# Moving part of the last layer's dense sums into the attention pass ahead of it

## The chip, the cores and the metric

One Trainium2 (trn2) chip, of which the kernel uses one core. Its engines are TensorE (PE; its weight loads are listed as PEld), VectorE (DVE), ScalarE (ACT), GpSimdE (POOL) and SyncE (SP), which issues the plain DMAs. The metric is the device time of one execution in microseconds; the median of the runs counts. Names such as L2227 are lines of the kernel before; in the changed kernel the lines behind the edit are up to 54 higher.

## The reference

Four layers of a graph network run over 6250 nodes of 256 features and 100000 random edges (`src`, `dst`, sorted by `dst`); after each layer the result is added to its input and normalised. Layers 0 and 1 are a mean aggregation and a dot-product attention. What bears on the change are the last two:

```python
# layer 2, twice: graph attention with 4 heads (edges and self-loops), exact GELU after each
h = (h_in @ W).reshape(n, Hh, Cc)
e = leaky_relu(alpha_s[src] + alpha_d[dst], 0.2)
alpha = softmax of e over the edges of each dst
out = segment_sum(h[src] * alpha[:, :, None], dst, n).reshape(n, Hh * Cc) + b
# layer 3, the last
msg_sum = segment_sum(x[src], dst, n)
cnt = segment_sum(ones, dst, n)
mean = msg_sum / maximum(cnt, 1.0)[:, None]
sage = mean @ W_l.T + b_l + x @ W_r.T
out = relu(relu(sage) @ W_ln.T + x)
# around each layer
x = _layernorm(x + layer(x))
```

## The kernel before

**Blocks.** The nodes form NB = 50 blocks of B = 125. The edges are laid out by target block, CM = 16 chunks of 128 edges each, with a few overflow chunks shared by 25 blocks (SH = 2). A *piece* is 4 chunks of one block in the attention passes (200 pieces a pass) and 6, 6 or 4 chunks in the last layer.

**The passes of layer 2.** `for layer in range(2)` runs two attention passes, the *first* and the *second pass* in the text. For each piece POOL gathers the rows of the source nodes from a table in DRAM (`gather`, L929, ten buffers `g`), DVE and ACT make the edge weights (L2152 to L2157) and scale the rows (L2160), DVE makes one-hot matrices of the targets (L938), and PE adds the rows into their targets (L2227). Once per block `keys2` makes one-hot columns `kb` on ACT (L947, L948) and spreads the targets' scores over the edges with 48 matmuls of 4 columns (L2185). `finish2` ends each pair of blocks. In the second pass it writes the new `x` times `W_l` as three bfloat16 parts to `x_table`, and, for the first ND = 24 blocks, `x` times `W_r` plus the bias, turned, to `xr_columns` (the *own-weight columns*).

**The last layer.** Its first 24 target blocks are summed densely: `a_table` holds, for each source node, a byte for each of 3000 targets, the count of edges between the two. `dense` walks over three groups of 8 target blocks (d = 0, 1, 2) and over the source blocks in pairs. For each pair it loads the rows of `x_table` (`xs`) and the counts of 1000 targets (`few`), ACT widens the counts to bfloat16 (`cnt`, L2343), and PE adds up: 3 parts x 2 halves of the features (DK = 2) x 2 *quarters* (q) of RW = 500 targets = 12 matmuls of 500 columns for each source block (L2393). At the end of a group `group3` multiplies by `rdeg_row` (one over the degree), adds the own-weight columns and hands over to `pair3`, which multiplies by `W_ln`. The other 26 target blocks (24 to 49) go by pieces with gathers from `x_table` (`piece3`, L929 and L963), among the dense steps.

**Where the counts come from.** `count_edges` makes `a_table` during the two passes of layer 2, with one-hot matrices on DVE (L1995) and matmuls of 500 columns (L2005); for each source block ACT evacuates two words of 1500 targets (L1981, L1982), both into one buffer `a_row`, which one store takes to DRAM.

**Order.** PE, DVE and ACT run in the order in which the program records them (`manual_schedule`); POOL and SP take theirs from the framework. The work of all pieces in flight is interleaved by *turns* (`Turns`): each piece, key block and finish is a generator that names the group in which it goes on. After turn t of a pass, `beside_2(t)` advances the counting:

```python
begin, until = (12 if layer == 0 else 0), len(made) - 12
share = COUNT_STEPS * (0.52 if layer == 0 else 0.5) / (until - begin)
```

In the last layer `beside_3` advances `dense` by RATE steps (yields of 12 matmuls) a turn, two for each pair of source blocks:

```python
RATE = 2 * len(order) / (0.9 * len(made))
```

with 75 pairs in `order` and 78 pieces in `made`. `LEAD` = 3 pairs are loaded ahead.

Of the kernel before, what the change touches and what calls it, by code (L numbers as in the profile page):

```python
# [17 lines left out]
P = 128  # L18
# [638 lines left out]
def gnn_stack_kernel(ctx: ExitStack, tc: tile.TileContext, ins, out):  # L657
# [33 lines left out]
    DK = D // P  # L691
# [21 lines left out]
    ND, RB, WORD = 24, 4, 3  # L713
    RW, NR = RB * B, ND // RB
# [10 lines left out]
    DC = max(c + n for _, c, n, _, _ in slots)  # L725
    COUNT_STEPS = NB * len(slots)
# [16 lines left out]
    with ExitStack() as fast:  # L743
# [47 lines left out]
        x_table = dram.tile([N, 3 * D], BF16, name="x_table_f")  # L791
# [837 lines left out]
        with tc.tile_pool(name="f0", bufs=1) as pool, tc.tile_pool(name="f0w", bufs=2) as work, tc.tile_pool(  # L1629
            name="f0v", bufs=1  # L1630
# [316 lines left out]
        def count_edges():  # L1947


            column = ap.tile([P, RW], F16, name="a_column", bufs=1)  # L1950
            nc.vector.scalar_tensor_tensor(
                column.rearrange("p (b n) -> p b n", n=B), iota[:, :RB, None].to_broadcast([P, RB, B]), float(B),
                iota_p[:, None, :B].to_broadcast([P, RB, B]), op0=ALU.mult, op1=ALU.add,
            )
            end, over = (
                ap.tile([P, 3, RW], BF16, name="a_hot", bufs=4).rearrange("p i j -> p (i j)").bitcast(F32)[:, : NB * DC]
                .rearrange("p (b c) -> p b c", c=DC) for _ in range(2)
            )
            nc.vector.tensor_copy(end, idx_s[:, :, :DC])
            unit = [ap.tile([P, NB, DC], F32, name=f"a_unit{w}", bufs=1) for w in range(NW)]  # L1960
            nc.vector.memset(unit[0], 1.0)
            for w in range(1, NW):
                nc.vector.memset(unit[w], 0.0)
            less = ap.tile([P, NB, DC], F32, name="a_less", bufs=1)
            nc.vector.tensor_copy(less, end)
            for r in range(1, NR + 1):
                nc.vector.tensor_single_scalar(over, end, float(r * RW), op=ALU.is_ge)
                nc.vector.scalar_tensor_tensor(less, over, -float(RW), less, op0=ALU.mult, op1=ALU.add)
                for w, by in ((r // WORD, 256.0 ** (r % WORD)), ((r - 1) // WORD, -(256.0 ** ((r - 1) % WORD)))):
                    if w < NW:  # L1970
# [3 lines left out]
            sts, rows, accs, hots, done = {}, {}, {}, {}, []  # L1974
            for k in range(len(steps) + 4):
                if done and done[0][2] <= k:
                    s, w, _ = done.pop(0)
                    if w == 0:
                        rows[s] = ap.tile([B, ND * B], U8, name="a_row", bufs=1)
                    word = ap.tile([B, RW], I32, name="a_word", bufs=1)  # L1980
                    nc.scalar.copy(word, accs.pop((s, w))[:B])  # L1981
                    nc.scalar.activation(  # L1982
                        rows[s][:, w * WORD * RW : (w + 1) * WORD * RW].rearrange("p (q j) -> p q j", q=WORD),
                        word.bitcast(U8).rearrange("p (j q) -> p q j", q=4)[:, :WORD, :], AF.Copy,
                        accum_out=counted[:B, s * NW + w : s * NW + w + 1],
                    )
# [12 lines left out]
                if 0 <= k - 1 < len(steps):  # L1999
                    s, w, c0, n, first, last = steps[k - 1]  # L2000
                    hot = hots.pop(k - 1)
                    if first:
                        accs[s, w] = apsum.tile([P, 512], F32, name="a_acc", bufs=2)[:, :RW]
                    for i in range(n):
                        nc.tensor.matmul(  # L2005
                            accs[s, w], sts[s][:, c0 + i, :], hot[:, i, :], start=(first and i == 0),
                            stop=(last and i == n - 1),
                        )
# [6 lines left out]
        counting = count_edges()  # L2015


        biases = [load_row(pool, ins[f"L2_gnn_b{i}"], f"bias{i}") for i in range(2)]
# [10 lines left out]
        for layer in range(2):  # L2029
# [7 lines left out]
            def finish2(b, layer):  # L2037
# [40 lines left out]
                else:  # L2078
# [164 lines left out]
            def beside_2(t):  # L2243
                if layer == 0 and t == 12:
                    next(counting)
                for _ in range(counts(t)):
                    next(counting, None)

            with tc.manual_schedule(engines={ENG.PE, ENG.DVE, ENG.Activation}):
                run_pass(turns, [(lambda a=a: piece2(*a)) for a in made], beside_2, keys2)  # L2250
                if layer:
                    for _ in counting:
                        pass


# [4 lines left out]
        with tc.tile_pool(name="f3g", bufs=5) as gp, tc.tile_pool(name="f3w", bufs=2) as work, tc.tile_pool(  # L2260
# [68 lines left out]
            order = [(d, s) for d in range(ND // (2 * RB)) for s in range(0, NB, 2)]  # L2329
            LEAD = 3  # L2330

            def load(k):
                d, s = order[k]
                xs = work.tile([B, 2, 3 * D], BF16, name="xs", bufs=LEAD + 1)
                move(nc.sync, xs, block_rows(x_table, s, 2))
                few = work.tile([B, 2, GW], U8, name="few", bufs=LEAD + 1)
                rows = a_table[s * B : (s + 2) * B, d * GW : (d + 1) * GW]
                move(nc.sync, few, rows.rearrange("(n p) d -> p n d", p=B))
                return xs, few

            def wide_counts(few):
                cnt = work.tile([B, 2, GW], BF16, name="cnt", bufs=3)
                nc.scalar.copy(cnt, few)  # L2343
                return cnt

            def pair3(b, sT, at):
# [26 lines left out]
            def dense():  # L2373
                loads = {k: load(k) for k in range(LEAD)}
                nexts = [wide_counts(loads[0][1])]
                for k, (d, s) in enumerate(order):
# [12 lines left out]
                    for i in range(2):  # L2389
                        for j in (2, 1, 0):  # L2390
                            for h in range(DK):
                                for q in range(2):
                                    nc.tensor.matmul(  # L2393
                                        accs[h][q], xs[:, i, j * D + h * P : j * D + (h + 1) * P],
                                        cnt[:, i, q * RW : (q + 1) * RW], start=(s + i == 0 and j == 2),
                                        stop=(s + i == NB - 1 and j == 0),
                                    )
# [85 lines left out]
```

## Time and profile before

| what | value |
|---|---|
| runs | 5936.43 us median of 3 (5924.23 to 5954.35) |
| profiled execution | 5892.39 us, span 5890.5 us |
| mean granted TensorE clock | 0.836 |
| PE, DVE, ACT, POOL busy | 4107.0, 3632.0, 2948.2, 3595.0 us |
| gathers (L929) of one attention pass | 800 |
| dense matmuls of the last layer (L2393) | 1800, 403.7 us busy |
| first, second attention pass, last layer | from about 2770, 3960, 5170 us |

The profile is of one execution. A group of instructions is read as: line, engine, operation, output <- inputs, shapes, count | busy us, mean ns of one | idle time of the engine just before them and what ended it. "issue" is time in which the engine waited for nothing that the profile shows. A line of a stretch gives busy us and the number of instructions of PE, PEld, DVE, ACT and POOL, then granted clock, DMA share and GB/s. Matmuls are pipelined: their mean duration overlaps, so that busy time by count gives the cost of one in a row.

### The profile page before, as it was taken

What the parts mean: (1) busy time and instruction counts of PE and PEld (TensorE: products, weight loads), DVE (VectorE), ACT (ScalarE), POOL (GpSimd) and SP (SyncE); (2) the same over time, 40 slices, a digit from 0 to 9 for tenths busy, and PEclk for the clock granted to TensorE, in tenths of its full rate; (3) what the DMA queues carried; (4) which work ended last, traced back from release to release, by engine and by line L of the source; (5) the groups of instructions that cost most, each with busy time, mean ns of one, the idle gap of its engine ahead of it and who ended that gap; (6) DMA issues with size and microseconds to landing.
All of it is one profiled execution on the core that took longest, in us unless ns stands there. A gap on an engine that the chain in (4) does not pass through costs nothing. (4 is left out here: it accounts for less than half of the span.)

```text
span 5890.5 us, 79635 instructions
## 1 busy us (share of the span) xinstructions
PE 4107.0 (70%) x25027; PEld 3010.6 (51%) x25027; DVE 3632.0 (62%) x9526; ACT 2948.2 (50%) x7453; POOL 3595.0 (61%) x3710
## 2 busy tenths in 40 slices
PE   0567788875777777773666766656776677769996
PEld 0355666663555566552554554544555555535554
DVE  7786666653767777773656656645766667613454
ACT  4015676882666676662454445533555555422331
POOL 5776666654666666653666666646666666556663
PEclk9788899997888888886777788777878878889998
DMA  6555565554666777763444444434545455477883
GB/s 157 141 165 159 157 158 155 153 149 143 204 204 206 208 211 210 207 189 86 132 135 134 135 137 136 133 101 123 146 139 140 138 147 140 118 197 221 235 238 102
DMA packets 409642, 940.75 MB, mean 160 GB/s; under 512 B 96973, under 2 KB 214331, under 8 KB 409211
## 3 DMA queue, kind: packets, MB, share of 16 engines
q0 software_dynamic: 221184, 670.83, 41.3%
q1 hardware_dynamic: 188026, 264.74, 15.3%
q8 instruction: 201, 3.29, 0.2%
q14 instruction: 231, 1.88, 0.1%
HBM read 848.02 MB, written 87.21 MB: 159 GB/s over the span
## 5 line engine op out<-in xcount | busy, mean ns | idle before, releaser
L929 POOL DMA_INDIRECT g<-hs_table_f,idx_d x1600 | 1527.6, 955 | 920.5 <-issue 453.1
L929 POOL DMA_INDIRECT g<-h_table_f,idx_d x800 | 802.0, 1002 | 435.2 <-issue 212.3
L2227 PE MATMUL ps<-g,st 128*125 128x260 f32 x3200 | 955.0, 445 | 116.6 <-issue 108.9
L929 POOL DMA_INDIRECT g<-kv_table_f,idx_s x784 | 744.8, 950 | 448.8 <-issue 289.4
L2160 DVE TENSOR_TENSOR g<-g,iota_p 128x1024 f32<-128x1024 f32 x400 | 488.4, 1221 | 654.6 <-ACT iota_p L2156 312.4
L2227 PEld LDWEIGHTS ps<-g,st 128*125 128x125 f32 x3200 | 712.7, 224 | 320.9 <-issue 151.0
L2185 PE MATMUL pe<-ad_parts,kb 125*128 125x4 bf16 x4800 | 220.1, 165 | 631.7 <-issue 543.1
L963 PE MATMUL ps<-g,st 128*128 128x256 bf16 (+1 forms) x3648 | 525.2, 300 | 136.3 <-issue 61.3
L929 POOL DMA_INDIRECT g<-x_table_f,idx_d x416 | 397.8, 956 | 289.3 <-issue 158.8
L963 PEld LDWEIGHTS <-st 128*128 128x128 bf16 x4104 | 427.8, 106 | 283.1 <-issue 130.3
L2185 PEld LDWEIGHTS <-kb 125*128 125x128 bf16 x4800 | 185.0, 99 | 721.8 <-issue 603.4
L1920 PE MATMUL ps<-g,st 128*125 128x264 f32 x1600 | 470.2, 442 | 28.1 <-issue 20.2
L947 ACT ACTIVATE kb<-kb,minus 125x512 bf16<-125x512 bf16 x600 | 426.2, 711 | 58.3 <-DMA g<-kv_table_f,idx 20.4
L948 ACT ACTIVATE kb<-kb,ones 125x512 bf16<-125x512 bf16 x600 | 432.6, 721 | 20.6 <-ACT kb L947 1.5
L2393 PE MATMUL d<-cnt,xs 125*128 125x500 bf16 x1800 | 403.7, 378 | 36.5 <-issue 20.4
L938 DVE TENSOR_TENSOR st<-iota_p,key_d 128x500 f32<-128x500 f32 (+1 forms) x550 | 410.6, 747 | 0.0
L1920 PEld LDWEIGHTS ps<-g,st 128*125 128x125 f32 x1600 | 344.9, 220 | 112.3 <-issue 28.9
L1903 DVE TENSOR_TENSOR prod<-g,qe 128x1024 f32<-128x1024 f32 x200 | 243.2, 1216 | 246.5 <-PE ps L1920 96.7
L2156 ACT ACTIVATE iota_p<-r 128x16 f32<-128x16 f32 (+2 forms) x504 | 90.9, 180 | 591.0 <-DVE e L2152 217.6
L1889 PE MATMUL qe<-q,kb 125*128 125x256 bf16 x2400 | 324.0, 288 | 65.6 <-issue 32.5
L1515 ACT ACTIVATE ob<-t_f,s_f 125x128 bf16<-125x128 f16 x800 | 310.3, 388 | 96.1 <-remote 65.1
L1889 PEld LDWEIGHTS <-kb 125*128 125x128 bf16 x2400 | 247.8, 103 | 141.6 <-issue 77.6
(458 smaller groups left out, 8051.4 us busy)
## 6 DMA issues: line engine op xcount, KB each, us to landing
kb<-keys_d_f SPq DMA_DIRECT2D x100, 448.0 KB
g<-hs_table_f,idx_d POOLq DMA_INDIRECT x1600
xs<-x_table_f SPq DMA_DIRECT2D x75, 336.0 KB
kb<-keys_s_f SPq DMA_DIRECT2D x50, 448.0 KB
a_table_f<-a_row SPq DMA_DIRECT2D x50, 328.1 KB
few<-a_table_f SPq DMA_DIRECT2D x75, 218.8 KB
g<-h_table_f,idx_d POOLq DMA_INDIRECT x800
g<-kv_table_f,idx_s POOLq DMA_INDIRECT x784
```

The costliest lines, as they stand in the source:

```text
L929: nc.gpsimd.indirect_dma_start(out=g, out_offset=None, in_=table, in_offset=bass.IndirectOffsetOnAxis(ap=idx, axis=0))
L938: nc.vector.tensor_tensor(st, iota_p[:, None, :w].to_broadcast([P, n, w]), key[:, :, None].to_broadcast([P, n, w]), op=ALU.is_equal,)
L947: nc.scalar.activation(part, part, AF.Square, bias=minus[:B])
L948: return nc.scalar.activation(part, part, AF.Relu, bias=ones[:B, 0:1], scale=-1.0)
L963: nc.tensor.matmul(ps[:, :m], st[:, i, :], g[:, i, k * D : k * D + m], start=(c0 + i == 0 and k == 2), stop=(c0 + i == CH - 1 and k == 0),)
L1515: nc.scalar.activation(ob[:, i, :], o1[:, i, :], AF.Copy, scale=val_b[:, at])
L1889: nc.tensor.matmul(qe[:, i, :], ts[:, c0 + i, :], q[:, k * D : (k + 1) * D], start=(k == 0), stop=(k == 2))
L1920: nc.tensor.matmul(sums[b][:B, : D + H1], hot, m[:, i, D - H1 :], start=(c == 0), stop=(c == CM - 1))
L2160: nc.vector.tensor_mul(feats, feats, pp[:, :, :, None].to_broadcast([p, n, H2, C2]))
L2185: nc.tensor.matmul(pe[:, c, :], ts[:, c, :], ad_parts[:, b, k, :], start=(k == 0), stop=(k == 2))
L2227: nc.tensor.matmul(sums[b][:B, : D + H2], hot, m[:, i, : D + H2], start=False, stop=(c == CM - 1))
L2393: nc.tensor.matmul(accs[h][q], xs[:, i, j * D + h * P : j * D + (h + 1) * P], cnt[:, i, q * RW : (q + 1) * RW], start=(s + i == 0 and j == 2),
```

## The change

- `first_sums`, a new generator, makes the dense sums of the first 500 targets (target blocks 0 to 3: d = 0, quarter 0) over source blocks 0 to 39 (AHEAD = 40) in the second pass: from turn 138 on, in three turns of five, one step loads the rows of a source block from `x_table` (for every third step also the counts of three source blocks from `a_table`), ACT widens one block's counts, and PE makes 6 matmuls. What is left when the pass has ended follows in a row. Then DVE multiplies by one over the degree, adds the own-weight columns of these targets and two stores put the sums back into `xr_columns`. `ready` keeps a step from running ahead of the stores of `x_table`.
- The counting has to be done by then: it gets 0.56 in place of 0.52 of its steps in the first pass, and in the second its steps lie in the first 136 turns in place of 188.
- Counts leave in halves: a buffer (of two) and a store for each word.
- In the last layer quarter 0 of group d = 0 starts at source block 40. Before it a pair of source blocks has 12 matmuls, loads the counts of one quarter only, and counts as one step. RATE follows.

```diff
-                        rows[s] = ap.tile([B, ND * B], U8, name="a_row", bufs=1)
+                    row = ap.tile([B, WORD * RW], U8, name="a_row", bufs=NW)
...
-                    if w == NW - 1:
-                        move(nc.sync, a_table[s * B : (s + 1) * B, :], rows.pop(s))
+                    move(nc.sync, a_table[s * B : (s + 1) * B, w * WORD * RW : (w + 1) * WORD * RW], row)
...
+        ready, AHEAD = [0], 40
+        def first_sums():
+            accs = [apsum.tile([P, 512], F32, name="a_acc", bufs=2)[:, :RW] for _ in range(DK)]
+            row = ap.tile([P, NB, DC], F32, name="a_less", bufs=1).rearrange("p b c -> p (b c)")[:, :RW]
+            nc.sync.dma_start(out=row, in_=rdeg_row[:, :RW].to_broadcast([P, RW]))
+            own = []
+            for h in range(DK):
+                own.append(ap.tile([P, NB, DC], F32, name=f"a_unit{h}", bufs=1).rearrange("p b c -> p (b c)")[:, :RW])
+                nc.sync.dma_start(out=own[h], in_=xr_columns[:, h, :RW])
+            few, xs, cnt = {}, {}, {}
+            for k in range(AHEAD + 2):
+                if k < AHEAD:
+                    while ready[0] <= k:
+                        yield
+                    if k % WORD == 0:
...
+                        move(nc.sync, part[:, :n, :], rows.rearrange("(n p) d -> p n d", p=B))
...
+                    hot = ap.tile([P, 3, RW], BF16, name="a_hot", bufs=4).rearrange("p i j -> p (i j)")
+                    xs[k], cnt[k] = hot[:B, : 3 * D], hot[:B, 3 * D : 3 * D + RW]
+                    move(nc.sync, xs[k], block_rows(x_table, k))
+                if 0 <= k - 1 < AHEAD:
+                    nc.scalar.copy(cnt[k - 1], few.pop(k - 1))
+                if k >= 2:
+                    part, by = xs.pop(k - 2), cnt.pop(k - 2)
+                    for j in (2, 1, 0):
+                        for h in range(DK):
+                            nc.tensor.matmul(
+                                accs[h], part[:, j * D + h * P : j * D + (h + 1) * P], by,
+                                start=(k == 2 and j == 2), stop=(k == AHEAD + 1 and j == 0),
+                            )
+                yield
+            for h in range(DK):
+                nc.vector.tensor_mul(accs[h], accs[h], row)
+                nc.vector.tensor_add(own[h], own[h], accs[h])
+                nc.sync.dma_start(out=xr_columns[:, h, :RW], in_=own[h])
...
+                    ready[0] = b + 2
...
-            begin, until = (12 if layer == 0 else 0), len(made) - 12
-            share = COUNT_STEPS * (0.52 if layer == 0 else 0.5) / (until - begin)
+            begin, until = (12, len(made) - 12) if layer == 0 else (0, len(made) - 64)
+            share = COUNT_STEPS * (0.56 if layer == 0 else 0.46) / (until - begin)
+            start = len(made) - 62
...
+                if layer and t == start:
+                    for _ in counting:
+                        pass
+                if layer and t >= start and (t - start) % 5 < 3:
+                    next(adding, None)
...
+            def quarters(d, s):
+                return (0, 1) if d or s >= AHEAD else (1,)
...
-                rows = a_table[s * B : (s + 2) * B, d * GW : (d + 1) * GW]
-                move(nc.sync, few, rows.rearrange("(n p) d -> p n d", p=B))
+                at = quarters(d, s)[0] * RW
+                rows = a_table[s * B : (s + 2) * B, d * GW + at : (d + 1) * GW]
+                move(nc.sync, few[:, :, at:], rows.rearrange("(n p) d -> p n d", p=B))
...
-                                for q in range(2):
+                                for q in quarters(d, s):
...
-                        yield ended
+                        if i or len(quarters(d, s)) == 2:
+                            yield ended
...
-            RATE = 2 * len(order) / (0.9 * len(made))
+            RATE = (2 * len(order) - AHEAD // 2) / (0.9 * len(made))
```

More of the change, by code (lines that the diff above doesn't have):

```diff
@@ L1973, in count_edges @@
             steps = [(s, *slot) for s in range(NB) for slot in slots]
-            sts, rows, accs, hots, done = {}, {}, {}, {}, []
+            sts, accs, hots, done = {}, {}, {}, []
             for k in range(len(steps) + 4):
@@ L1977, in count_edges @@
                     s, w, _ = done.pop(0)
-                    if w == 0:
-                        rows[s] = ap.tile([B, ND * B], U8, name="a_row", bufs=1)
+                    row = ap.tile([B, WORD * RW], U8, name="a_row", bufs=NW)
                     word = ap.tile([B, RW], I32, name="a_word", bufs=1)
@@ L1982, in count_edges @@
                     nc.scalar.activation(
-                        rows[s][:, w * WORD * RW : (w + 1) * WORD * RW].rearrange("p (q j) -> p q j", q=WORD),
+                        row.rearrange("p (q j) -> p q j", q=WORD),
                         word.bitcast(U8).rearrange("p (j q) -> p q j", q=4)[:, :WORD, :], AF.Copy,
@@ L2015, in gnn_stack_kernel @@
         counting = count_edges()
+        ready, AHEAD = [0], 40
[13 more added lines that the diff above has]
+                    if k % WORD == 0:
+                        n = min(WORD, AHEAD - k)
+                        part = ap.tile([B, WORD * RW], U8, name="a_row", bufs=NW).rearrange("p (n d) -> p n d", n=WORD)
+                        rows = a_table[k * B : (k + n) * B, :RW]
+                        move(nc.sync, part[:, :n, :], rows.rearrange("(n p) d -> p n d", p=B))
+                        for i in range(n):
+                            few[k + i] = part[:, i, :]
+                    hot = ap.tile([P, 3, RW], BF16, name="a_hot", bufs=4).rearrange("p i j -> p (i j)")
[16 more added lines that the diff above has]
+                nc.sync.dma_start(out=xr_columns[:, h, :RW], in_=own[h])
@@ L2018, in gnn_stack_kernel @@
+        adding = first_sums()
         biases = [load_row(pool, ins[f"L2_gnn_b{i}"], f"bias{i}") for i in range(2)]
@@ L2251, in gnn_stack_kernel @@
                 if layer:
-                    for _ in counting:
+                    for _ in adding:
                         pass
@@ L2336, in load @@
                 few = work.tile([B, 2, GW], U8, name="few", bufs=LEAD + 1)
-                rows = a_table[s * B : (s + 2) * B, d * GW : (d + 1) * GW]
-                move(nc.sync, few, rows.rearrange("(n p) d -> p n d", p=B))
-                return xs, few
+                at = quarters(d, s)[0] * RW
+                rows = a_table[s * B : (s + 2) * B, d * GW + at : (d + 1) * GW]
+                move(nc.sync, few[:, :, at:], rows.rearrange("(n p) d -> p n d", p=B))
+                return xs, few[:, :, at:]
             def wide_counts(few):
                 cnt = work.tile([B, 2, GW], BF16, name="cnt", bufs=3)
-                nc.scalar.copy(cnt, few)
+                at = GW - few.shape[-1]
+                nc.scalar.copy(cnt[:, :, at:], few)
                 return cnt
@@ L2391, in dense @@
                             for h in range(DK):
-                                for q in range(2):
+                                for q in quarters(d, s):
                                     nc.tensor.matmul(
                                         accs[h][q], xs[:, i, j * D + h * P : j * D + (h + 1) * P],
-                                        cnt[:, i, q * RW : (q + 1) * RW], start=(s + i == 0 and j == 2),
+                                        cnt[:, i, q * RW : (q + 1) * RW], start=(s + i == (0 if d or q else AHEAD) and j == 2),
                                         stop=(s + i == NB - 1 and j == 0),
```

## The prediction

> **What bounds the kernel now.** I read the page first, then stretches of each engine's busy time, then waits and groups by stage, then the order of the instructions at the seams.
>
> ```profile
> PE 4107.0 (70%) x25027; PEld 3010.6 (51%) x25027; DVE 3632.0 (62%) x9526; ACT 2948.2 (50%) x7453; POOL 3595.0 (61%) x3710
> ...
> PE   0567788875777777773666766656776677769996
> ...
> PEclk9788899997888888886777788777878878889998
> DMA  6555565554666777763444444434545455477883
> ```
>
> The first line is an average over stages and decides nothing. The slices do: the last layer (from slice 35, 5170 us) is the one stage with PE at 9 and DMA at 8; the two attention passes ahead of it (2770 to 3900 and 3960 to 5160 us) show PE at 6 and 7. The chain that ended last holds only the last 7 us ("issue 0%"), so I go by stretches: 1000 us inside each pass, then the first 100 us of the last layer, then its rest.
>
> ```profile
> 2824.00:3824.00 1000.00, 682.29 (x4263) 510.18 (x4263) 606.70 (x1470) 498.90 (x1114) 645.82 (x681) 0.79 0.49 135
> 4016.00:5016.00 1000.00, 709.31 (x4351) 518.60 (x4350) 679.79 (x1779) 514.41 (x1177) 647.24 (x676) 0.80 0.50 139
> 5184.00:5284.00 100.00, 72.73 (x361) 37.06 (x361) 7.59 (x36) 19.96 (x14) 60.23 (x64) 0.81 0.79 221
> 5284.00:5814.00 530.00, 508.16 (x2944) 299.80 (x2942) 218.45 (x978) 157.86 (x150) 331.87 (x347) 0.99 0.79 224
> ```
>
> Columns: PE, PEld, DVE, ACT, POOL busy, granted clock, DMA share, GB/s. In the last layer PE is busy 508 of 530 us: it is the bound, except for the first 100 us. In the second pass it is busy 709 of 1000, and this view tells what the rest is (4000 to 4740 us):
>
> ```profile
> PE pe L2185 <- issue: 136.1, 126, 2.6
> PE ps L2227 <- issue: 55.9, 69, 2.0
> PE a_acc L2005 <- issue: 12.5, 12, 1.7
> ```
>
> These 204.5 us are nearly all of PE's idle time there (213 of 740), and no semaphore ends them. So either PE is full in the pass (busy and "issue" make 99%), or these holes are slack. The whole forecast hangs on that. The two passes decide: the second has 27.0 us more PE work per 1000 us than the first (709.31 against 682.29), yet its gathers fall only from 681 to 676, 0.74% or 7.4 us. From the times of line 2044 a block of 125 targets takes 23.68 us in the first pass and 23.76 in the second (blocks 5 to 45), 0.08 for 27.0 x 0.0237 = 0.64 us of PE work. So 0.13 to 0.27 of added PE work came out as time; the holes shrank for the rest. POOL paces: its gathers follow each other at 1.25 us while nothing holds them (0.95 busy, 0.30 "issue"), 20 of the 23.7 us, and in the order of the trace it halts at the first gather of about half the pieces, where a buffer is to come free, and nowhere else.
>
> **The change part by part.** The prices, from groups of the second pass (first line) and the last layer:
>
> ```profile
> L2005 PE MATMUL a_acc<-a_hot,a_st 128*128 128x500 bf16 x331 | 99.6, 402 | 16.9 <-issue 13.7 <-DVE st L938 1.5 <-DVE r L2154 1.5
> ...
> L2393 PE MATMUL d<-cnt,xs 125*128 125x500 bf16 x1800 | 403.7, 378 | 36.5 <-issue 20.4 <-ACT cnt L2343 15.4
> L929 POOL DMA_INDIRECT g<-x_table_f,idx_d x416 | 397.8, 956 | 289.3 <-issue 158.8 <-PE ps L963 59.7 <-remote 34.4
> ...
> L2343 ACT CAST cnt<-few 125x2000 bf16<-125x2000 uint8 x75 | 139.2, 1857 | 266.8 <-issue 126.5 <-PE d L2393 67.2 <-DMA few<-a_table_f 30.7
> ```
>
> *Removed from the last layer*: 40 blocks x 3 parts x 2 halves = 240 of the 1800 dense matmuls, at 403.7 / 1800 = 0.224 us: **-54 us** where PE is the bound. ACT's casts shrink as well and were idle before them; that is worth nothing. Next late is POOL: 420 gathers x 1.25 = 525 us in a stage of 631 us (5184 to 5815), so it still fits into 577.
>
> *Added to the second pass*: in the built order 216 of the 240 matmuls stand among its pieces 137 to 198, 24 behind it; 30 counting matmuls go to the first pass (333 to 303 here, 367 to 397 there). Net 186 x 99.6/331 = 0.301 us: 56 us of PE work. By the measured ratio 0.13 this is **+7 us** (0.27: 15; nothing hidden, and the holes growing in proportion: 56 / 0.709 = 79; below nothing is excluded by little: DVE and ACT lose the counting in the last 62 turns, say -5). I take 0.13, from the periods, as they leave out the ragged ends. The 30 in the first pass: 9 us, **+1** (0 to 9 / 0.682 = 13). Beside them: 40 casts on ACT (about 0.56 us, as line 1981's 125x500), 22 us in some 360 where ACT is half idle; the counting that leaves that stretch frees more. Counting now ends at piece 128, not 178, so DVE carries a third more of it per turn: 117.3 us (line 1995) over 1160 us become some 107 over 750, 4 points on 68%: hidden. SP gets 40 loads of 192 KB and 14 of up to 188 KB, two issues each at about 0.4 us, 43 us; the loads of keys and own rows behind them are made 8 and some 5 turns ahead, which covers it; the DMA share goes from 0.50 to about 0.60. The count rows leave in two stores with a buffer each, which ends ACT's wait at line 1982 (50.6 us, 13 times); ACT idles anyway: 0.
>
> *The seam* is where moved steps are bare. Four steps of sums (24 matmuls), three casts, four DVE operations and two stores stand behind the last products, and SP's first loads, DVE's first one-hots and PE's first dense matmul now wait for those stores to land. Before:
>
> ```profile
> 5184.53 6.55 PE L2393 MATMUL d<-cnt,xs 125*128 125x500 bf16 x24 [15.45 <-ACT cnt L2343]
> 5190.92 2.13 PE L963 MATMUL ps<-g,st 128*128 128x256 bf16 x18
> ...
> 5206.25 0.58 PE L2393 MATMUL d<-cnt,xs 125*128 125x500 bf16 x1 [2.90 <-issue]
> ```
>
> PE is free from 5169.1. The casts follow ACT's last on xp (5171.9), so three of the steps begin after 5172.5; 24 matmuls after an idle time took 6.55 us: end about 5179. DVE 4 x 0.68 (lines 2364, 2365): 5181.5. A store lands in 2.4 us (x_table's last, 5173.0 to 5175.5): 5184, when SP may go on; before, it went on at 5175.8. That is **+8 us** (0 to 11): the low end because the gathers do not wait for it and PE lost some 20 us from 5195 to 5219 anyway, as the last quoted line shows (one matmul each 1 to 3 us, while DMA was at 0.97 and 0.74 of its time).
>
> *Bunched loads*: the first 20 pairs of blocks now count as one step each, so they pass at 1.85 pairs a turn, not 1.07, in the first 11 turns. A turn then moves 1.85 x (384 + 125 KB) + 5.33 gathers x 197 KB = 2.0 MB in 7.4 us, 270 GB/s; 224 GB/s went with a share of 0.79, so that is 0.95. I take **+4 us**; the bounds are 0 (it fits) and 22 (those 80 us go as the first 100, 73% busy instead of 96% and more).
>
> Here a rule speaks against the change. Row: the packet records of 4016 to 5016 us have 500-byte packets at 0.030 us, 1000-byte ones in the last layer at 0.058 to 0.062, so 500 bytes cost half; but those 500-byte rows are writes. The Trainium skill (DMA: Bandwidth & Descriptors, Specifications) says that under 512 bytes a transfer misses line rate. By it, the halved count rows (500 bytes) would save nothing in the bunched turns, 2.2 MB' worth, 7.9 us a turn instead of 7.4: an estimate of 5 us more, and a sum of -29. No run here shows 500-byte reads.
>
> **Sum**: -54 + 7 + 1 + 8 + 4 = **-34 us**. The profiled execution took 5892.4 us (span 5890.5, 1.9 around it), 44 below the median 5936.4 of the runs; I carry the difference over: **5902 us**, -0.6%.
>
> **The rivals.**
> *PE is full in the second pass* (the other side). One mechanism: the "issue" holes are part of PE's work and grow with it. For it: busy and "issue" make 99%, and no engine ends the holes. Against: the passes' ratio of 0.13 to 0.27. Price: 79 + 13 + 8 + 4 - 54 = +50: 5986 us. The sum is nil when 65 us of work in the passes cost 42 (a ratio of 0.65), and slower by 0.5% when they cost 72 (1.1).
> *The last layer gives it back*: DMA at 0.95 and POOL at 20.2 of 22.2 us a block (577 / 26) hold PE, as in the first 100 us. For it: those 27 lost us, and the passes' 2 to 3 us over POOL's own time per block. Against: after 5284 PE waits for DMA in no group. Price: bunched loads 22 instead of 4: -16, 5920 us.
> *It doesn't move what it says*: excluded but for the 24 matmuls, by the built order.
>
> **How the numbers follow.** A measurement of this kernel can tell about 0.5% from no change, 30 us here. My forecast has 0.62 (two thirds of that beyond -30, as its sum lies 4 us past the bound, and the ends of its terms reach from -54 - 5 = -59 to -54 + 15 + 2 + 11 + 15 = -11), the last layer giving back 0.18, PE full 0.20. Faster 0.43; same 0.20 + 0.17 = 0.37; slower 0.20. Range: 5880 (-56, all but nothing lost) to 5982, nearly to the full-PE case; its own range would be 5880 to 5925.
>
> **What would show it.** Right: the last layer from the first dense matmul to the last gather takes about 50 us less with PE still near 96%; the second pass keeps its 23.8 us a block in blocks 34 to 49, with "issue" before line 2185's matmuls (now 2227) shrunk; the first dense matmul 8 us later after the last product than before. Wrong: blocks 34 to 49 at 26 us or more, "issue" grown; or PE idle in the first 100 us of dense sums above 30 us; or ACT's casts ended by DMA of the counts.

## The result, and the profile after

The changed kernel takes 5960.28 us (median of 14 runs) against 5940.56 for the kernel before on the same chip (14 runs): a ratio of 1.0027, interval 1.0016 to 1.0038. By the ratio it is slower by some 16 us (the medians differ by 20), where 34 us faster was forecast. The profiled execution took 5968.1 us (span 5966.3). The profiled execution of before, at 5892.4, was 0.5% under the fastest of the 14 runs, so the two traces are compared by stages and not by their ends.

The page of the changed kernel, its busy times and its slices:

```profile
PE 4119.7 (69%) x25027; PEld 3001.0 (50%) x25027; DVE 3640.1 (61%) x9530; ACT 2951.7 (49%) x7493; POOL 3584.9 (60%) x3710
...
PE   0567788774677777763676666655777777769896
...
PEclk9788999997888888886778778877888778889998
DMA  5555555554666666663454444434545455478773
```

The last layer (slices 35 to 38) has PE at 9, 8, 9 where before it had 9, 9, 9: PE was given less to do there and idles more. The stretches that the prediction read (1000 us of each pass, the first 100 us of the last layer, its rest), with the same columns:

```profile
2865.00:3865.00 1000.00, 668.41 (x4228) 503.69 (x4227) 615.12 (x1488) 496.44 (x1109) 638.56 (x673) 0.79 0.48 134
4073.00:5073.00 1000.00, 719.33 (x4375) 516.08 (x4374) 660.81 (x1722) 513.67 (x1177) 635.42 (x664) 0.81 0.51 144
5258.00:5358.00 100.00, 71.41 (x371) 38.40 (x372) 14.52 (x77) 19.45 (x21) 62.66 (x67) 0.81 0.89 234
5358.00:5888.00 530.00, 476.86 (x2676) 278.28 (x2675) 214.14 (x956) 143.52 (x143) 327.92 (x344) 0.95 0.77 219
```

In the 530 us PE is busy 477 instead of 508, at a granted clock of 0.95 instead of 0.99, yet GpSimd has issued 344 gathers where it issued 347. The work went, the time stayed: from the first gather of the last layer to its last it is 642.8 us before and 644.9 after. The groups of the last layer (PE, then GpSimd):

```profile
L2446 PE MATMUL d<-cnt,xs 125*128 125x500 bf16 x1560 | 364.3, 387 | 43.5 <-issue 25.5 <-DMA xs<-x_table_f 17.5
L963 PE MATMUL ps<-g,st 128*128 128x256 bf16 x1170 | 152.8, 283 | 36.2 <-issue 25.0 <-DVE st L2362 9.3 <-DMA g<-x_table_f,idx_d 1.8
...
L929 POOL DMA_INDIRECT g<-x_table_f,idx_d x416 | 396.6, 953 | 295.0 <-issue 114.6 <-PE a_acc L2046 51.6 <-PE ps L963 44.7
```

Dense matmuls take 39.4 us less than before (364.3 against 403.7), and PE's idle time grew, most of it "issue". GpSimd's row is that of before to 2% (397.8 busy, 289.3 idle).

To say where the 54 us went, I took each step of PE in the last layer, from one matmul's start to the next one's, off its kind's usual step at full clock (0.2135 us for a dense matmul, 0.109 for one of a piece). What is over is "half clock" (a step of up to twice its usual length), a wait that a semaphore ended, or "issue". In us, on the chips where the kernel before takes 5941 to 5951 (one trace of each kernel or run):

| kernel | first gather to first dense | first to last dense | usual steps | "issue" | half clock |
|---|---|---|---|---|---|
| before | 7.8 | 632.6 | 562.6 | 45.6 | 11.2 |
| counting moved only | 8.2 | 621.7 | 562.6 | 33.2 | 11.7 |
| all additions, last layer as before | 20.0 | 612.8 | 562.6 | 25.2 | 11.1 |
| changed | 17.4 | 624.3 | 511.7 | 67.7 | 26.9 |
| changed, again | 18.6 | 619.9 | 511.7 | 69.9 | 21.1 |
| changed, third | 18.2 | 616.7 | 511.7 | 72.0 | 21.7 |

What is missing to the time from the first to the last dense matmul, 11 to 18 us in each row, are the waits that a semaphore ended. The traces of these chips hold only a third of all semaphore updates (last section), so the line between such a wait and "issue" is rough.

The usual steps fall by 51 us, as the removal promised. The holes and the half clock together are 36 to 57 us in the three kernels with 1800 dense matmuls and 91 to 95 in the changed one, and its first dense matmul comes 10 us later.

### The profile page after: what moved, and what is told of

It is laid out like the page before. It is cut to its first block, busy times and chain, and to the rows that moved or that the text cites. A ratio compares the mean times of both kernels' runs of the same rounds, so it can differ in the third digit from the quotient of the medians.

```text
span 5966.3 us, 80107 instructions
## 1 busy us (share of the span) xinstructions
PE 4119.7 (69%) x25027; PEld 3001.0 (50%) x25027; DVE 3640.1 (61%) x9530; ACT 2951.7 (49%) x7493; POOL 3584.9 (60%) x3710
## 5 line engine op out<-in xcount | busy, mean ns | idle before, releaser
L2446 PE MATMUL d<-cnt,xs 125*128 125x500 bf16 x1560 | 364.3, 387 | 43.5 <-issue 25.5
```

Of the source, the lines that this page charges most:

```text
L2446: nc.tensor.matmul(accs[h][q], xs[:, i, j * D + h * P : j * D + (h + 1) * P], cnt[:, i, q * RW : (q + 1) * RW], start=(s + i == (0 if d or ...
```

## The experiments

The theories: **A**, the forecast's, PE's work bounds the last layer; **B**, its gathers pace it, whatever PE does; **C**, bunched loads eat the gain; **D**, the products moved into the pass cost their full time there.

The chips differ, which the runs showed at once and which decides the reading. On one kind the kernel before takes 5941 to 5951 us (the slower chips from here on; the result above is from one of them), on the other 5067 to 5074 (the faster). Four chips are on record for the experiments: 8 and 10 are slower ones, 4 and 9 faster ones, and chip 4 was so at two different times. Each ratio is to the kernel before on the same chip.

**The skip alone** (faster chip):

```
 # dense(), kernel before; quarters() as in the change, AHEAD = 40, no first_sums
-for q in range(2):
+for q in quarters(d, s):
...
-RATE = 2 * len(order) / (0.9 * len(made))
+RATE = (2 * len(order) - AHEAD // 2) / (0.9 * len(made))
```

> The kernel before with the last layer's half of the change alone: the 240 dense matmuls are left out there and nothing makes their sums elsewhere (that part of the result is missing). Theory A, the forecast's: PE bounds the last layer, so from its first gather to its last the stage falls from 642.8 us by 54 less some 4 for the bunched loads, to about 593, and the whole kernel is some 50 us (0.84%) faster than before. Theory B, the gathers pace it: GpSimd issues the 420 gathers of the stage at 1.53 us each whatever PE has to do (642.8 / 420, as in the three other gather stages of before: 1.55, 1.53, 1.52); the stage stays within 8 us of 642.8 and the kernel within 0.15% of before. Theory C, the bunched loads eat the gain: the stage loses time in its first 200 us (DMA share over 0.88 there, against 0.79), and gains after it; sum near nothing as well, but the gathers 128 to 416 come at less than 1.45 us each.

Measured: 5032.5 us against 5068.6, ratio 0.9937 (0.9923 to 0.995). 36 us faster: two thirds of theory A's sum, so PE's work does bound the stage on this chip, if not alone. B is out here: the stage takes 556.0 us, 1.32 us a gather. By the reckoning of the table: usual steps 511.5 us from the first dense matmul to the last, 541.9 in all, "issue" 0.1, half clock 8.3; the rest are waits for semaphores.

**Few dense matmuls** (faster chip first):

```
 for q in range(2):
+    if s + i not in (0, NB - 1) and (j, h, q) != (0, 0, 0):
+        continue
     nc.tensor.matmul(
```

> The kernel before, with all loads and casts of the last layer, but only 216 of its 1800 dense matmuls (the first and the last source block's all, one of twelve of the others); the rest of the products is left out of the result. 1584 x 0.224 = 355 us of PE work are gone, PE has some 250 us left. Theory A (PE bounds): the stage falls from 642.8 us to what GpSimd needs when nothing holds it, 420 x 1.25 = 525 us, or a little more. Theory B (gathers pace at 1.53 us whatever PE does): 642.8 stays within 20 us. A result between, 550 to 610, would say that part of the 0.28 us over 1.25 are GpSimd's own halts and part come from PE.

Measured: 4988.2 us, ratio 0.9845 (0.9827 to 0.9863); the stage falls to 529.8 us, 1.26 us a gather: GpSimd's own 1.25, as A has it. So taking dense matmuls away can give at most about 80 us on the faster chip.

**Half of the gathers, without and with the skip** (faster chip first):

```
-for i in reversed(range(n)):
+for i in reversed(range(n // 2)):
     gather(g[:, i, :], x_table[:, :], idx_d[:, b, c0 + i : c0 + i + 1])
...
 # the products of a piece: column i % (n // 2) of g in the place of i
```

> The kernel before, with half of the gathers in the last layer (each gathered column used twice, so the neighbour sums of that layer are not the reference's); all its matmuls stay. This takes GpSimd and half of the gathers' traffic out of the way. Theory A: PE's own work holds the stage, some 606 us of matmuls (403.7 dense + 147.3 pieces + 55 others); it stays at 610 to 643 us. Theory B says no more than that PE's work is a floor below the gathers' pace: also 606 or a little more, not below. Read together with the next run, which takes the 240 matmuls out of this kernel.

> The half-gather kernel and the 240 dense matmuls left out of it. With the gathers out of the way PE must be the bound under every theory: 54 us less than the half-gather kernel. Theory A then expects the same 54 less in the run with all gathers; theory B expects the 54 here and nothing there, which would show that the gathers, not PE, decide what the removal is worth. Theory C (bunched loads): less than 35 here, as the loads of the first 20 pairs are bunched in this run too.

Measured: half of the gathers 5066.1 us, ratio 0.9997 (0.9987 to 1.0007): no change. With the skip 5014.9 (two runs), ratio 0.9897 (0.9879 to 0.9915): 51 us less, the whole price of the 240 matmuls. With all gathers the skip had given 36.

**The changed kernel and its parts** (slower chip). The parts are the change without the skip (the last layer as before), and that without first_sums too:

```
 # sums, no skip: quarters() and its uses replaced by the lines of before
 # counting only: besides that
-if layer and t >= start and (t - start) % 5 < 3:
-    next(adding, None)
...
-for _ in adding:
+for _ in counting:
     pass
```

> The changed kernel once more, beside its parts on one chip. The chip of the first runs and that of the last call differ: the kernel before took 5941 us on the one and 5069 on the other, where PE has no hole that ends in "issue" (261 of 1000 us of the second pass on the first chip, none on the other). Theory A (PE bounds the last layer; the holes of the first chip are PE's instructions coming late, which spreads into every stage): on a chip without the holes the skip is worth 36 us as measured, and the additions in the pass and the seam cost 10 to 16, so 20 to 26 us faster, about 5045. On a chip with the holes: 16 to 20 us slower, as before. Theory D (what is added in the second pass costs its full 56 us wherever the pass runs): slower by 20 to 30 on either chip.

> Only the counting is moved (30 counting products to the first pass, the rest ended 50 pieces earlier in the second, the count rows stored in halves): no sums in the pass, the last layer as before. Theory A: within 5 us of before on a chip without the holes, 0 to +10 with them. If it costs more than 10, the moved counting and not the sums is what the pass pays for.

> The changed kernel with the last layer of before: the 240 products are made twice, in the pass and again in the last layer (that part of the sums counts double). Its difference from before is the price of all additions: the moved counting, 216 products in the second pass, 24 and the stores in the seam. Theory A: 10 to 16 us on a chip without PE's holes (7 + 1 from the passes, 8 from the seam; the bunched loads are not in this run), 15 to 35 with them. Theory D: 55 to 70 on either.

Measured: the changed kernel 1.0030 (1.0020 to 1.0040), counting only 1.0006 (0.9994 to 1.0018), with the sums 1.0013 (1.0001 to 1.0025). In us of 5947: counting 4, sums and seam 4 more, the skip with its bunched loads another 10, where it should have paid; by the intervals each of these differences is uncertain by 7 to 10 us. D (55 to 70 for the additions) is out: they cost 8.

**Even steps** (slower chip):

```
-if i or len(quarters(d, s)) == 2:
-    yield ended
+yield ended
...
-RATE = (2 * len(order) - AHEAD // 2) / (0.9 * len(made))
+RATE = 2 * len(order) / (0.9 * len(made))
```

> The changed kernel, but each of the first 20 pairs of blocks again counts as two steps of the last layer's schedule, so that its loads are not bunched in the first 11 turns: 1.07 pairs a turn throughout as before, and fewer products per turn at first. Theory C (bunched loads cost what the removal gains): 15 to 25 us faster than the changed kernel. Theory A: PE lacks work in the first turns and has it later, so the removal is worth less; 5 to 20 us slower than the changed kernel on a chip without the holes.

Measured: 1.0008 (0.9997 to 1.0018), 0.0022 or 13 us better than the changed kernel beside it (4 to 22 by the two intervals). So C is right in its sign, nearly so in its size, and wrong as the whole reason: with the loads spread, the skip is worth 0.0005 or 3 us against the run with the sums and no skip (-6 to 12 by the two intervals), not 54.

**Few dense, half gathers, half gathers with the skip, and the changed kernel, on a slower chip**, which separates A from B there:

> Again the kernel with 216 of the last layer's 1800 dense matmuls, all loads and casts kept (most of the dense products are left out of the result). On the chip where the kernel before takes 5069 us it made the gathers of the stage follow at 1.26 us and the whole 79 us faster. On a chip where it takes 5940: theory B (a gather takes 1.49 to 1.57 us there in every stage, whatever PE has to do) expects 1.5 us a gather still, 630 us for the stage, and less than 20 us off the total. Theory A (PE's own work sets the pace, its holes included) expects the stage near 530 us and about 110 us off. A result between says that the holes are paid by the matmul, and how much of the stage they make.

> Again half of the last layer's gathers, all matmuls (its neighbour sums are not the reference's). On the faster chip: no change, PE without a hole in the stage (nominal 562 us of matmul steps in 578). On a chip with the holes: if gathers in flight make PE's holes (theory B: the holes grow and shrink with what the gathers leave), the 25 to 46 us of "issue" in the stage fall under 10 and the stage to about 590, some 45 us off the total. If the holes are PE's own (theory A), they stay and so does the time, within 10 us.

> Again half of the gathers and the 240 dense matmuls left out. On the faster chip 51 us less than with half of the gathers alone. On a chip with the holes: theory B expects 40 to 54 less than the run with half of the gathers, as with the gathers out of the way PE is the bound there too; theory A's holes would take some 30 of the 54 back, as in the changed kernel ("issue" 25 to 46 us in three kernels with 1800 matmuls, 64 to 70 in three with 1560).

> The changed kernel a third time, beside the others of this call. On a chip with the holes: 0.2 to 0.4% slower than before, as twice. On a chip without: the skip alone gave 36 us there, the additions cost 4 to 16, so 20 to 32 us (0.4 to 0.6%) faster than before.

Measured: few dense matmuls 0.9991 (0.9980 to 1.0003), no change with 1584 of 1800 matmuls gone. Half of the gathers 0.9918 (0.9898 to 0.9938), 44 us of 5951. Half of the gathers and the skip 0.9837 (0.9816 to 0.9858), another 48 (two runs of each of these two). The changed kernel 1.0018 (1.0006 to 1.0031). The last layer of the few-dense kernel on this chip, as a stretch (columns as above) and as GpSimd's group; then the group of the same kernel on the faster chip:

```profile
5243.00:5869.00 626.00, 337.29 (x1734) 218.20 (x1734) 234.40 (x1047) 178.40 (x166) 402.32 (x420) 0.72 0.80 229
```

```profile
L929 POOL DMA_INDIRECT g<-x_table_f,idx_d x416 | 398.9, 959 | 277.7 <-issue 174.9 <-remote 65.8 <-PE ps L963 21.9
```

```profile
L929 POOL DMA_INDIRECT g<-x_table_f,idx_d x416 | 398.1, 957 | 156.8 <-issue 148.3 <-DMA g<-x_table_f,idx_d 4.6 <-PE ps L963 1.5
```

PE is busy for 337 of 626 us, and still a gather takes 1.5 us; with all 1800 matmuls the stage is 638 to 643 us in the traces of these chips. This is B, on this chip. With half of the gathers the holes go (by the reckoning of the table "issue" 6.2 us, usual steps 562.5 of 586.7), PE becomes the bound, and the skip is worth its 48 us. What PE idles for "issue" before dense matmuls then (5240 to 5840 us; 20.4 us in the kernel before), and GpSimd's group, which now waits for PE:

```profile
PE d L2398 <- issue: 4.8, 5, 1.7
```

```profile
L929 POOL DMA_INDIRECT g<-x_table_f,idx_d x208 | 201.0, 966 | 439.3 <-PE ps L2323 337.5 <-issue 92.2 <-PE pd L925 5.9
```

**Seven buffers for the gathered rows**, to see whether GpSimd's halts come from the loop through five of them (all five runs fell on the faster chip):

```
-tc.tile_pool(name="f3g", bufs=5)
+tc.tile_pool(name="f3g", bufs=7)
```

> The kernel before with seven buffers of gathered rows in the last layer, not five. Loop theory (GpSimd halts as a buffer comes back late): GpSimd may be 37 gathers ahead, not 27, so the first 100 us gain, the halts of the rest shrink until PE itself is the bound: its nominal steps are 562 us of the 633, so up to 40 us off (0.7%), 10 to 30 likely. Other theory (gathers and loads in flight slow PE down, the loop only passes it on): the halts stay, as PE is some 27 us behind the landed rows anyway; within 8 us of before.

> The few-dense kernel (216 of 1800 dense matmuls in the last layer, the rest left out of the result) with seven buffers. Loop theory: the stage falls from 626 us to 540 to 580, as a halt of 2 to 4 us at a piece of 6.7 to 7.5 us is covered by two more pieces. Other theory: 615 to 630, a gather still at 1.5 us.

> The changed kernel with the even steps (1.0008 of before last time) and seven buffers. Loop theory: it is the one that can use the 51 us taken from PE, 30 to 60 us faster than before, and faster than the kernel before with seven buffers. Other theory: within 10 us of before.

> The few-dense kernel with seven buffers again (most dense products of the last layer left out). On the faster chip 4989 us as before. On a chip as in the first runs: loop theory 540 to 580 us for the stage (626 with five buffers); other theory 615 to 630, a gather still at 1.5 us.

> The kernel before with seven buffers again. On the faster chip no change, as measured. On a chip as in the first runs: loop theory 10 to 30 us off; other theory within 8 us of before.

Measured: the kernel before with seven buffers 0.9998 (0.9989 to 1.0007) and 1.0004 (0.9995 to 1.0013); few dense 0.9845 and 0.9839, as with five; the changed kernel with even steps and seven 0.9988 (0.9979 to 0.9997). Buffers are worth nothing on the faster chip. On the slower ones it wasn't tried, and what holds a gather there stays open. The even steps, which gain 13 us on a slower chip, gain nothing here: with them (and seven buffers) 0.9988, the changed kernel as it is 0.9962 on another of the faster chips (next), some 13 us apart and the other way round, as theory A expected of a chip without the holes.

**The changed kernel on the faster chip:**

> The changed kernel itself. On the faster chip: the skip alone took 36 us off; the pass costs 2 (second pass 1024.5 us from its first gather to its last with the sums in the run with even steps and seven buffers, 1022.5 without) and the seam 9 (first dense matmul 16.8 us after the first gather, 7.5 without): 25 us off, 0.5%, 5042. On a chip as in the first runs 0.2 to 0.3% slower, as three times.

Measured: 5055.7 us against 5073.5, ratio 0.9962 (0.9948 to 0.9975), 18 us faster. The forecast's direction holds there, at about half of its size. The last layer takes 569.1 us from its first gather to its last, against 556.0 with the skip alone and 580.9 in the kernel before with seven buffers. What it loses of the skip's gain goes with the seam, in which the first dense matmul comes 22.1 us after the first gather (6.4 with the skip alone). The pass costs nothing that can be seen: 1022.6 us from its first gather to its last, against 1025.0 in the kernel before with seven buffers on the same chip. No version was found that beats both kernels on both chips.

## Why the prediction was wrong, point by point

**The step that failed is the first term, "-54 us where PE is the bound", with the line that let it pass: "420 gathers x 1.25 = 525 us", which "still fits".** PE is busy 96% of the last layer before, and I took that for the bound. The 51 us of usual steps did go; as time they are worth 3 us on the slower chips (even steps against no skip), 36 on the faster, and 48 to 51 on either with half of the gathers gone. And 1.25 us is what a gather takes while nothing holds it; on the slower chip something holds it in every stage, and with 1584 of the 1800 dense matmuls gone the 420 gathers still take 626 us. The rows that spoke against it were on the page of before. First, here beside the skip-alone kernel's page, taken on the faster chip (busy us, mean ns, idle before them):

```profile
L929 POOL DMA_INDIRECT g<-hs_table_f,idx_d x1600 | 1527.6, 955 | 920.5 <-issue 453.1
L929 POOL DMA_INDIRECT g<-h_table_f,idx_d x800 | 802.0, 1002 | 435.2 <-issue 212.3
L929 POOL DMA_INDIRECT g<-kv_table_f,idx_s x784 | 744.8, 950 | 448.8 <-issue 289.4
L929 POOL DMA_INDIRECT g<-x_table_f,idx_d x416 | 397.8, 956 | 289.3 <-issue 158.8
```

```profile
L929 POOL DMA_INDIRECT g<-hs_table_f,idx_d x1600 | 1530.3, 956 | 547.0 <-issue 403.7
...
L929 POOL DMA_INDIRECT g<-h_table_f,idx_d x800 | 801.9, 1002 | 292.6 <-issue 220.6
L929 POOL DMA_INDIRECT g<-kv_table_f,idx_s x784 | 742.3, 947 | 241.1 <-issue 160.7
```

Busy and idle over the count give 1.53, 1.55, 1.52 and 1.65 us a gather in the four stages of before (1.53 in the last without its wait of 49 us at the seam). PE is busy 66 to 71% of the first three and 96% of the last. A pace that four stages share at such different loads of PE is hardly PE's; the run with few dense matmuls shows that it isn't. I used the same fact in the passes, where added work vanishes in holes, and not in the last layer, where by the same holes removed work buys nothing. On the faster chip the same gathers take 1.30, 1.37 and 1.25.

**The second pass, +7 us (0 to 79): right.** By their gathers the second pass's blocks 34 to 49 take 23.7 us in the counting-only run and 24.0 to 24.3 in the five traces with the sums: 0.3 to 0.6 x 16 = 5 to 9 us for 56 us of PE work. On the faster chip nothing can be seen: from its first gather to its last the pass takes 1023.5 us with the sums and 1022.5 without on chip 9, 1022.6 and 1025.0 on chip 4. The expectation of the last run had 1024.5 against 1022.5, but the one figure reached to the last gather's end and the other to its start. The rows of the pass on the two chips, the changed kernel in both:

```profile
L2269 PE MATMUL ps<-g,st 128*125 128x260 f32 x1321 | 399.7, 445 | 63.9 <-issue 60.7 <-DMA g<-hs_table_f,idx_d 2.9
...
L2227 PE MATMUL pe<-ad_parts,kb 125*128 125x4 bf16 x1968 | 85.0, 165 | 165.3 <-issue 164.3 <-ACT g L2199 0.6
```

```profile
L2269 PE MATMUL ps<-g,st 128*125 128x260 f32 x1536 | 444.7, 441 | 58.5 <-DVE st L938 46.1 <-issue 9.4 <-ACT a_word L1980 3.0
...
L2227 PE MATMUL pe<-ad_parts,kb 125*128 125x4 bf16 x2304 | 81.8, 165 | 99.4 <-ACT kb L948 99.2
```

Before the matmuls of 4 columns (line 2227, 2185 before) PE idles for "issue" on the slower chip (207.8 us in before's 1000, 164.3 here: it shrank, as forecast, while all of PE's idle time fell from 291 to 281) and for ScalarE's one-hots on the faster. The prediction's ground, "no semaphore ends them", was weaker than it looked, as the trace lacks two thirds of the semaphore updates; but the holes are not hidden waits. Of each 12 matmuls that read one set of one-hots, PE idles on the faster chip only before the first (279 us in all with the skip alone); on the slower one 153 us before the first and 479 before the other eleven, which have nothing left to wait for. The rival "PE is full in the second pass" is out on both: its 79 us came out as 9 at most.

**The first pass, +1:** with the rest of the moved counting 4 us, interval -4 to 11; right within what can be measured.

**The seam, +8 us (0 to 11): right in size.** From the end of the last product to the first dense matmul 15.4 us before, 24.9 to 26.1 in the changed kernel's three traces: +10. After (the last sums of the pass, then the first dense matmul):

```profile
5246.86 3.96 PE L2046 MATMUL a_acc<-a_hot 125*128 125x500 bf16 x18 [2.14 <-ACT a_hot L2041]
5268.36 4.60 PE L2446 MATMUL d<-cnt,xs 125*128 125x500 bf16 x12 [17.55 <-DMA xs<-x_table_f]
```

On the slower chips the gathers don't wait for it, so little of it becomes time: 4 us with the sums and all. On the faster chip it is what the skip's gain is lost to.

**Bunched loads, +4 us (0 to 22): too low, within its bounds.** Spreading them gave 13 (4 to 22). The first 200 us of the last layer, the changed kernel (DMA share 0.89 and 0.92, against 0.79 and 0.80 before):

```profile
5258.00:5358.00 100.00, 71.41 (x371) 38.40 (x372) 14.52 (x77) 19.45 (x21) 62.66 (x67) 0.81 0.89 234
5358.00:5458.00 100.00, 88.11 (x493) 51.22 (x492) 33.98 (x146) 28.16 (x28) 62.58 (x67) 0.95 0.92 257
```

Here PE idles 12 us of 100 in the second stretch, where before it idled 2 (97.85 busy). That idle time is not the price by itself: with even steps PE idles still more (29.5 us of the first 100 after the first dense matmul, 20.2 in the changed kernel), and the kernel is faster. Of ScalarE's idle time before the casts of counts 54.5 us end with the loads, 30.7 before. The Trainium skill's rule (DMA: Bandwidth & Descriptors, Specifications: under 512 bytes a transfer misses line rate) was weighed against the rows: the 500-byte reads, which now have a trace, take 0.036 us in the first 100 us, against 0.062 for 1000 bytes in the same stretch of before. That is 0.58 for half the bytes, so the rule shows faintly. As an estimate, the last layer's 5000 such reads at 0.005 us over half of 0.062, on 16 DMA engines, are some 2 us of the 13.

**The rival "the last layer gives it back"** (0.18, 5920 us) was right in its place and far too mild in its price: it let bunched loads take 22 of the 54, and all but some 3 are lost even with the loads spread. Its ground against, "PE waits for DMA in no group", looked for the wrong mark. Gathers that are too slow did not show as PE waiting for them, since PE takes up a piece some 27 us (the median, before and after) after its last packet; they show as holes of "issue" (45.6 us before, 6.2 with half of the gathers), and in that the last layer is like the passes.

What the prediction said would show it: the last layer about 50 us shorter (it is 635 before and 628 after from the first dense matmul to the last gather), PE near 96% (it is 90), the pass under 26 us a block (24.3 at most), the first dense matmul 8 us later (10). The two in the last layer failed. Of the signs of being wrong, ScalarE's casts ended by the loads of the counts did show; PE idle above 30 us in the first 100 us of dense sums did not (20.2, before 26.7), nor did 26 us a block.

The 5960 us lie inside the range of 5880 to 5982, but by luck: the range reaches up there for the rival "PE is full in the second pass", which is out. The forecast's own range ended at 5925.

## What to carry to other kernels

A busy share of 96% is no proof of a bound. Ask for the pace of the stage's unit (here a gather) and whether other stages, with other loads, keep the same one; if they do, work taken off the busy engine may come back as holes, as it did here. Evidence that holes swallow added work is also evidence that they return when work is removed: use it on both sides of a move. And a change that is worth 18 us on one chip may cost 16 on another chip of the same model, so say which resource of the chip the gain rests on.

## What the runs showed of the hardware

- Two kinds of chip, 17% apart for one program: 5941 to 5951 us and 5067 to 5074 us, with the same mean durations of instructions (a gather 955 and 956 ns, a 128x260 product 445 and 442). The difference is idle time: on the slower ones PE idles 632 us before line 2185's matmuls in the whole run of before, 543 of it "issue"; on the faster, with the skip alone, 279 us, all but 0.4 of it for ScalarE's one-hots. Why the chips differ is open.
- The traces differ in kind too: a trace of a slower chip holds a third of the semaphore updates (33494 in before's, 102174 in that of the skip alone on the faster; of VectorE's 7494 there are 3992 and 7461). In a stretch of 400 us of the last layer (from 100 us after its first gather) 205 of VectorE's 493 are there, with half of the gathers 437 of 561. So "issue" on a slower chip can be a wait whose end is missing. Whether the lost records and the slowness have one cause isn't shown.
- On the slower chips an engine starts late behind PE, and it goes with the gathers. VectorE takes up a finished block of neighbour sums (line 2285) 1.15 us after the last product's recorded end in the median of 19 waits in before, 0.04 us with half of the gathers on a slower chip (20 waits) and 0.04 with the skip alone on the faster (16). A matmul's end is modelled in the records, so whether the matmul or its signal is late can't be told. Whether that lateness sets the 1.5 us of a gather isn't shown.
- A PE that idles more is granted less clock: in the last layer 0.95 in before, 0.72 with few dense matmuls on a slower chip (busy 337 of 626 us) and 0.78 on the faster (324 of 530). In the changed kernel's three traces steps at half clock rose from 88 to between 140 and 186, 21 to 27 us of time instead of 11.
